# Two steps of a hand-written order moved: the loads of a later pair of images, and the mean of a group norm

## The chip, the cores and the metric

The kernel runs on one core of one Trainium2 chip. The metric is device time in microseconds of one execution; before the change it is 2930.93 us, the median of 3 runs (2928.26 to 2932.24). The core's engines have their own instruction queues and run side by side: TensorE (PE; its weight loads, PEld, are listed apart), VectorE (DVE), ScalarE (ACT) and GpSimd (POOL). SyncE (SP) issues every data transfer (DMA) of this kernel.

## The reference, cut to what matters

The input is 64 images of 1024 channels, 14 x 14 pixels, in float32. Two bottleneck blocks follow each other. The first is three convolutions with batch norms. The second, with which the change is concerned, is for each image:

```
out = relu(group_norm(conv1x1(x, w1)))                 # 1024 -> 256 channels, "first norm"
om = conv3x3(out, w_off) + b_off                       # 27 channels: 18 offsets, 9 masks
sampled = bilinear_sample(out, grid + offsets) * sigmoid(om[:, 18:])
out = einsum('bckhw,ock->bohw', sampled, w2)           # 9 taps, 256 -> 256, "second conv"
out = relu(group_norm(out))                            # "second norm"
out = group_norm(conv1x1(out, w3))                     # 256 -> 1024, "third conv", "third norm"
return relu(out + x)
```

A group norm's mean and variance go over all pixels of an image and a group of channels (32 channels in the third norm). All 1024 channels are held as 8 blocks of 128 partitions.

## The kernel before, in words

The 64 images are worked on in 32 pairs (`NP`). The first bottleneck has three stages, one convolution each, for all pairs; its results go to DRAM (`h3`), one tensor for each pair. In the second bottleneck the pairs go through a pipeline written out by hand: `slot(t)` (L1783) lists the work of one turn as small steps in the list `todo`, and runs them at its end. Slot t holds work of several pairs at once:

- of pair t+1: `first_conv`, `first_norm`, `offset_conv` (L1162), `selection` (L1211), the transposes and `factors` (L1238);
- of pair t: `sampling`, on PE with copies on ACT, in two parts `sp[0]` and `sp[1]` (taps 0 to 4 and 5 to 8), and the second conv in two parts `pd[0]` (35 products) and `pd[1]` (28);
- of pair t-1: the second norm, the third conv `d3` (28 products) and the third norm, in three steps `mean`, `root`, `end`;
- of pair t-2 and t-1: the output, in halves, with `store` (L1746);
- of pair t+2: its loads, `load` (L1069), and `residual` (L1075), the end of the first bottleneck for that pair.

`put(steps, extra, at)` (L1765) places each step of `extra` ahead of the step of `steps` with the number in `at`; `weave` (L1760) mixes two lists evenly. In a full slot (t from 2 to 30) the order is: the first conv of t+1 with `extra` (among it, at place 6, the list `late`); then `sp[0]` woven with half of `d3`; then two products of `d3`, the six steps of the offset conv and the one of `selection` (`om`); then `sp[1]` woven with the rest of `d3`; then `pd[0]` with a second list `extra`, and `pd[1]` with a third.

What sets the order of instructions: the second bottleneck fixes by hand only PE's order, which is the order of the steps. For DVE, ACT, POOL and SP the program's scheduler lays out each queue ahead of time: of the instructions that it takes as ready it places the one that was traced first. An instruction in `tc.keep_in_program_order(...)` is pinned: it can't be placed ahead of the instruction that was traced last before it on its engine. It says nothing about what is traced after it. On the chip each queue then runs in its order.

The pieces that the prediction's steps touch:

- The third norm's statistics are bn_stats on DVE (L987). `stats(3)` at the end of `d3` issues the last four, and the very last is pinned. `Norm.mean` (L1005) sums them on DVE (`total`, L1003, tile `gn_0m`), multiplies the sum by a constant matrix on PE (L1012), copies the result (L1014, `gn_0gm`) and forms the variance's terms on DVE (L1019 to L1026, `gn_0v`). `Norm.root` (L1028) multiplies those on PE (L1031), adds epsilon on DVE (L1036) and takes the power on POOL (L1037).
- The second conv multiplies seven sums of inputs instead of eight. Products (5, k) read b22, (0, k) b11, (4, k) b21, then (1, k) b12, (2, k) b22, (3, k) b11, (6, k) b21, in that order; k goes over the taps. The sums are formed in place on DVE by `subtract` (L1466, profiled as L1467): `first_sum` (L1472) makes b12 - b11, pinned; behind product (5, 4), the fifth of `pd[0]`, comes b22 - b12; behind (4, 1) b22 - b11, behind (1, 1) b21 - b22.
- `load(p)` makes four DMAs on SP, each pinned: two of x (L196) into the buffer `Y[p % 4]`, two of `h3` (L204) into `Z0`. `residual(p)` reads both: eight DVE instructions (L216), pinned, and eight relus on ACT (L228).
- `selection` issues on SP: the offsets and the mask to DRAM (L1221, L1222, tile `dm`), then three transfers that read them back, spread over partitions (L1234, tiles `wt` and `mk`). `factors` reads these on DVE (L1246), and later sends `wd` (L1266).
- `output` adds x on DVE (L1724), takes the relu on ACT (L1726) and stores (L1752). The third conv of the next pair writes the same two z buffers: on POOL (L1652) and on DVE (L1656, L1660).

Of the kernel before, what the change touches and what calls it, by code (L numbers as in the profile page):

```python
# [44 lines left out]
def kernel(  # L45
# [20 lines left out]
    NP = B // 2  # L66
# [126 lines left out]
    def load_x(p, order=lambda ins: ins):  # L193
        for i in range(2):
            order(
                nc.sync.dma_start(  # L196
                    Y[p % 4][:, :, ts(i, HW)], x[2 * p + i].rearrange("(b p) q -> p b q", p=P)
                )
            )

    def load_h3(p, r, order=lambda ins: ins):
        for half in range(2):
            order(
                nc.sync.dma_start(  # L204
                    r[:, ts(half, HB)].rearrange("p b q -> p (b q)"), h3[p][:, ts(half, HB * N2)]
                )
            )
# [447 lines left out]
    with l0, tc.manual_schedule(  # L655
# [107 lines left out]
        for p in range(2, NP - 2, 2):  # L763
            tt = Ts
            for j in range(HB):
                acc = [ps.tile([P, N2], FP, tag=f"ps{m}", name=f"c3_{p}_{j}_{m}") for m in range(4)]
                part = ts(j, P)
# [156 lines left out]
    def build_second_bottleneck(l1, path, run, early):  # L924
# [141 lines left out]
        def start(p):  # L1066
            pairs[p] = {"y": Y[p % 4]}

        def load(p):  # L1069
            start(p)  # L1070

            load_x(p, tc.keep_in_program_order)
            load_h3(p, Z0, tc.keep_in_program_order)

        def residual(p):  # L1075

            for b in range(CB):

                tc.keep_in_program_order(end_of_first(p, Z0, b))
                relu_of_first(p, b)  # L1080
# [236 lines left out]
        def spread_rows(p, e):  # L1317

            q = pairs[p]
            k0, k1 = tapsets[e]  # L1320
            S = one.tile([QR, wide * KT[e % 2]], FP, tag=f"S{e % 2}", name=f"S_{p}_{e}")
            q["S"][e] = S
            for g, r0, piece in pieces(e):
                yield nc.sync.dma_start(
                    S[:, piece],
                    q["wd"][g][0, r0 : r0 + R, k0:k1, :]
                    .rearrange("r k n -> r (k n)")
                    .unsqueeze(1)
                    .to_broadcast([R, W, piece.stop - piece.start]),
                )  # L1330
# [36 lines left out]
        def corners(p, e):  # L1367

            q = pairs[p]
            S, X = q["S"][e], q["X"][e]  # L1370
            k0, k1 = tapsets[e]
            q["S"][e] = {}
            for g, r0, piece in pieces(e):

                tc.keep_in_program_order(
                    nc.vector.tensor_tensor(S[:, piece], S[:, piece], X(piece), ALU.mult)  # L1376
                )
                q["S"][e][g, r0] = S[:, piece].rearrange("q (k i n) -> q k i n", k=k1 - k0, i=2)
# [87 lines left out]
        def subtract(dst, a, b):  # L1466
            return nc.vector.tensor_tensor(dst, a, b, ALU.subtract)  # L1467

        def sevenfold(p):
            return shared and p < NP - 1  # L1470

        def first_sum(p, e):  # L1472

            if sevenfold(p):
                kt = tapsets[e][1] - tapsets[e][0]
                b11, b12 = (pairs[p]["sm"][e][:, 0, :kt, i] for i in range(2))

                tc.keep_in_program_order(subtract(b12, b12, b11))
# [238 lines left out]
        def output(p, half):  # L1717

            q = pairs[p]
            for b in range(half * HB, half * HB + HB, 2):  # L1720
                z = q["z"][half][:, ds(b % HB, 2)]

                tc.keep_in_program_order(
                    nc.vector.tensor_tensor(z, z, q["y"][:, ds(b, 2)], ALU.add)  # L1724
                )
                nc.scalar.activation(z, z, AF.Relu)  # L1726
            store(p, half * HB, half * HB + HB)
# [55 lines left out]
        def slot(t):  # L1783


            this, ahead, back = (0 <= n < NP for n in (t, t + 1, t - 1))
            E = len(tapsets)

            def part(yes, stage, *args):
                return stage(*args) if yes else []  # L1790


            front = ahead and not (early and t < 1)
            sp = [part(this, sampling, t, e) for e in range(E)]
            pd = [part(this, second_conv, t, e) for e in range(E)]
            d3 = part(back, third_conv, t - 1)

            for e in range(2, E):
                sp[e - 2].append(lambda e=e: this and (list(spread_rows(t, e)), list(spread_columns(t, e)), corners(t, e)))
            d1 = part(front and not (early and t < 2), first_conv, t + 1)  # L1800
            norm1, norm2, norm3 = (
                part(front, first_norm, t + 1)[2 if early and t == 1 else 0 :],
                part(back, second_norm, t - 1),
                part(back, third_norm, t - 1),
            )
            weights = [lambda e=e: corners(t, e) for e in range(2)] if this else []

            late = [lambda: output(t - 2, 1)] if t >= 2 else []
            if t + 2 < NP and not (early and t < 1):
                late.append(lambda: load(t + 2))  # L1810
            if this and not d1 and not early:
                weights[0]()
            if t == NP - 1:
                ends2 = second_norm(t)
            om = part(front, offset_conv, t + 1) + part(front, selection, t + 1)
            half = len(d3) // 2
            if d1:
                extra = list(zip((5, 8, 12, 12, 13, 13, 14), norm2)) + [(10, w) for w in weights[:1]]
                extra = sorted(extra + [(6, s) for s in late], key=lambda v: v[0])
                todo = put(d1, [s for _, s in extra], [k for k, _ in extra])  # L1820
                todo += put(weave(sp[0], d3[:half]), norm1, (4, 7, 14, 16, 18, 21))
                todo += weights[1:] + d3[half : half + 2] + om
                todo += weave(sp[1], d3[half + 2 :])
            else:
                extra = list(zip((3, 6, 8, 9, 10, 10, 10), norm2)) + list(zip((0, 0, 1, 1), norm1))
                extra = sorted(
                    extra + [(9, w) for w in weights[1:]] + [(4, s) for s in late], key=lambda v: v[0]
                )
                todo = put(sp[0], [s for _, s in extra], [k for k, _ in extra])
                todo += om + weave(sp[1], d3[:half]) + d3[half:]  # L1830
            more = t + 2 < NP and not (early and t < 1)

            scale = lambda k: k * len(pd[0]) // 35
            extra = [(4, s) for s in norm3[:1]] + ([(4, lambda: first_sum(t, 0))] if this else [])
            extra += list(zip((6, 11, 16, 21), part(ahead, transposes, t + 1)))
            extra += list(zip((12, 19), part(ahead, factors, t + 1)))
            extra += list(zip((10, 20), norm3[1:]))
            extra += [(20, lambda: first_sum(t, 1))] if this and E == 2 else []
            extra += [(21, lambda: residual(t + 2))] if more else []
            extra = [(scale(k), s) for k, s in extra]  # L1840
            extra.sort(key=lambda v: v[0])
            todo += put(pd[0], [s for _, s in extra], [k for k, _ in extra])
            for e in range(1, E - 1):
                todo += sp[e + 1] + pd[e]
            if ahead:
                todo += [lambda: list(spread_rows(t + 1, 0)), lambda: list(spread_columns(t + 1, 0))]
                todo += [lambda: list(spread_rows(t + 1, 1)), lambda: lend(t + 1)]
            if early and t == 0:
                todo.append(weight_sums)

            n = len(pd[E - 1])
            extra = []
            if early and t == 0:

                extra += list(zip((5, 8), first_norm(2)))
            if early and t + 1 in (1, NP - 1):
                extra.append((12, lambda: corners(t + 1, 0)))
            if back:
                extra.append((n * 18 // 28, lambda: output(t - 1, 0)))
            if t == NP - 1:  # L1860

                extra += list(zip([n // 2 + k for k in (3, 5, 6, 6)], ends2))
            extra.sort(key=lambda v: v[0])
            todo += put(pd[E - 1], [s for _, s in extra], [k for k, _ in extra])
            if ahead:
                todo.append(lambda: list(spread_columns(t + 1, 1)))
            if back and t == NP - 1:
                todo.append(lambda: output(t - 1, 1))
            for step in todo:
                step()  # L1870
# [176 lines left out]
```

## Time and profile before

| What | Value |
|---|---|
| time, median of 3 runs | 2930.93 us |
| profiled execution, its own time | 2930.46 us |
| span of that execution in the trace | 2928.7 us |
| busy: PE, weight loads, DVE, ACT, POOL | 96%, 70%, 80%, 46%, 34% |
| one slot, from mean to mean of the third norm (1922.38, 1981.69, 2040.45) | 59.3 and 58.8 us |
| queue of SP's transfers | 421.71 MB, 44.7% of 16 DMA engines' span |

All rows but the first come from one profiled execution. The span is the time between the first and the last event that the trace shows; the execution's own time is 1.8 us longer. In a row of the trace's timeline stand: start in us from the span's start, length in us, engine, line of the kernel, operation, output <- inputs, shape, number of instructions that are merged into the row, and in brackets idle time of the engine before it and what ended it. A product of the second conv is two records of PE. Tile names lose their buffer number. A waits row reads: engine, tile and line that waited <- what it waited for: microseconds in total, times, the longest. The records on PEld are the loads of the stationary operand, which can run while PE multiplies.

### The profile page before, as it was taken

What the parts mean: (1) busy time and instruction counts of PE and PEld (TensorE: products, weight loads), DVE (VectorE), ACT (ScalarE), POOL (GpSimd) and SP (SyncE); (2) the same over time, 40 slices, a digit from 0 to 9 for tenths busy, and PEclk for the clock granted to TensorE, in tenths of its full rate; (3) what the DMA queues carried; (4) which work ended last, traced back from release to release, by engine and by line L of the source; (5) the groups of instructions that cost most, each with busy time, mean ns of one, the idle gap of its engine ahead of it and who ended that gap; (6) DMA issues with size and microseconds to landing.
All of it is one profiled execution on the core that took longest, in us unless ns stands there. A gap on an engine that the chain in (4) does not pass through costs nothing.

```text
span 2928.7 us, 40983 instructions
## 1 busy us (share of the span) xinstructions
PE 2824.3 (96%) x13327; PEld 2053.4 (70%) x13327; DVE 2330.2 (80%) x5573; ACT 1336.8 (46%) x2723; POOL 988.9 (34%) x1065
## 2 busy tenths in 40 slices
PE   9999899999999889999999999999999999999986
PEld 5555555555555468878887888778877887788773
DVE  7877899997888758778877887787878787877764
ACT  0000222114555435555555556555655565556553
POOL 4621466654666112222222222222222222222221
PEclk9999999999999999999999999999999999999998
DMA  7665000005555444564456545554555455544521
GB/s 229 192 176 154 15 1 1 1 2 213 218 195 203 133 130 138 176 187 160 141 173 184 162 143 168 188 164 144 164 187 169 142 164 185 172 142 159 183 93 46
DMA packets 350436, 424.42 MB, mean 145 GB/s; under 512 B 27876, under 2 KB 292612, under 8 KB 349956
## 3 DMA queue, kind: packets, MB, share of 16 engines
q1 hardware_dynamic: 350212, 421.71, 44.7%
q8 instruction: 107, 1.75, 0.3%
q14 instruction: 117, 0.96, 0.1%
HBM read 296.63 MB, written 116.76 MB: 141 GB/s over the span
## 4 chain that ended last, share of the span: by engine, by line
PE 63%; DVE 19%; DMA 8%; ACT 3%; POOL 3%; issue 2%; SPq 1%; DVEq 0%; ACTq 0%; POOLq 0%
PE pd L1511 18%; PE c L389 10%; PE c L770 9%; PE sp L1396 6%; PE d L1092 6%; PE c L534 5%; DMA out_dram<-z 5%; PE d L1640 4%; DVE v L520 3%; DVE gn_0st L987 2%; DVE S L1376 2%; DMA X<-wd 1%; DVE V L1647 1%; DVE off L1207 1%; DVE X L1156 1%
## 5 line engine op out<-in xcount | busy, mean ns | idle before, releaser
L1396 PE MATMUL sp<-S,aT 126*128 126x420 f32 (+3 forms) x1536 | 494.7, 419 | 22.6 <-ACT sm L1404 13.0
L1511 PE MATMUL pd<-sm,w2b_sb 128*128 128x196 f32 x2232 | 408.6, 331 | 3.8 <-DVE sm L1467 3.8
L1404 ACT COPY sm<-sp 128x336 f32<-128x336 f32 (+3 forms) x640 | 285.6, 451 | 254.5 <-PE sp L1396 239.9
L1511 PEld LDWEIGHTS pd<-sm,w2b_sb 128*128 128x128 f32 x2232 | 370.6, 190 | 4.1 <-DVE sm L1467 4.1
L1092 PE MATMUL d<-h,w1b_sb 128*128 128x392 f32 x1024 | 358.0, 498 | 2.8 <-ACT h L228 2.8
L534 PE MATMUL c<-v,u_sb 128*128 128x392 f32 x1024 | 342.9, 497 | 10.4 <-DVE bn1sh L167 8.2
L1511 PE MATMUL pd<-sm,Sc 128*128 128x196 f32 x1674 | 315.5, 331 | 0.0
L534 PEld LDWEIGHTS c<-v,u_sb 128*128 128x128 f32 x1024 | 194.4, 191 | 158.9 <-DVE v L520 11.7
L1396 PEld LDWEIGHTS sp<-S,aT 126*128 126x128 f32 x1536 | 256.7, 191 | 47.0 <-ACT sm L1404 32.4
L1467 DVE TENSOR_TENSOR sm<-sm 128x980 f32<-128x980 f32 (+1 forms) x248 | 263.4, 1072 | 20.7 <-PE pd L1511 14.6
L1511 PEld LDWEIGHTS pd<-sm,Sc 128*128 128x128 f32 x1674 | 277.9, 190 | 0.2
L1092 PEld LDWEIGHTS d<-h,w1b_sb 128*128 128x128 f32 x1024 | 188.6, 190 | 121.0 <-ACT h L228 5.2
L1707 ACT ACTIVATE z<-z,gn_0sh,gn_0sc 128x196 f32<-128x196 f32 x496 | 222.5, 537 | 36.6 <-DVE gn_0sh L1053 36.6
L1037 POOL TENSOR_TENSOR gn_0sc<-gn_0sc,mhalf 128x16 f32<-128x16 f32 (+3 forms) x35 | 122.1, 3488 | 251.6 <-DVE gn_0sc L1036 242.3
L520 DVE TENSOR_TENSOR v<-t 128x392 f32<-128x392 f32 x256 | 193.1, 812 | 0.0
L1640 PE MATMUL d<-h,w3b_sb 128*128 128x196 f32 x744 | 180.4, 333 | 0.0
L1726 ACT ACTIVATE z<-z 128x784 f32<-128x784 f32 x124 | 103.1, 855 | 145.4 <-DVE z L1724 145.2
L1652 POOL TENSOR_TENSOR E<-V,E 128x196 f32<-128x196 f32 x124 | 74.4, 600 | 281.3 <-DVE V L1647 281.3
L1640 PEld LDWEIGHTS d<-h,w3b_sb 128*128 128x128 f32 x744 | 132.9, 189 | 50.4 <-issue 19.7
L1376 DVE TENSOR_TENSOR S<-S,X 126x840 f32<-126x840 f32 (+1 forms) x192 | 148.3, 822 | 24.1 <-DMA X<-wd 18.7
L1540 POOL TENSOR_TENSOR E<-V,E 128x196 f32<-128x196 f32 x31 | 18.8, 605 | 412.7 <-DVE V L1539 392.7
L987 DVE BATCH_NORM_STATS2 gn_0st<-z 128x6 f32<-128x196 f32 x504 | 153.2, 348 | 4.2 <-ACT z L1691 0.9
(842 smaller groups left out, 5147.3 us busy)
## 6 DMA issues: line engine op xcount, KB each, us to landing
xc<-in_x_dram SPq DMA_DIRECT2D x128, 392.0 KB
h<-o SPq DMA_DIRECT2D x64, 784.0 KB
h<-in_x_dram SPq DMA_DIRECT2D x64, 784.0 KB
h<-h SPq DMA_DIRECT2D x64, 784.0 KB
out_dram<-z SPq DMA_DIRECT2D x126, 392.0 KB
S<-wd SPq DMA_DIRECT2D x64, 413.4 KB
X<-wd SPq DMA_DIRECT2D x64, 413.4 KB
S<-wd SPq DMA_DIRECT2D x64, 330.8 KB
```

The source lines that it names most:

```text
L389: nc.tensor.matmul(acc[m], a, b, start=(j == 0), stop=(j == HB - 1))
L520: nc.vector.tensor_tensor(v[:, u].rearrange("p (i y x) -> p i y x", y=7, x=7), cols[c][:, :, i : i + 13 : 2, :], cols[c][:, :, j : j + 13 ...
L534: nc.tensor.matmul(m[u], u_sb[:, c, u, k % 4, ts(o, P)], vts[k][c][:, u], start=(c == 0), stop=(c == MB - 1),)
L770: nc.tensor.matmul(planes(acc[m]), a, b, start=start, stop=True, skip_group_check=True)
L987: last = nc.vector.bn_stats(self.st[:, b, i, :], src[:, ts(i, HW)])
L1092: nc.tensor.matmul(q["pt"][o], w1b_sb[:, c, ts(o, P)], q["y"][:, c, :], start=(c == 0), stop=(c == CB - 1),)
L1396: nc.tensor.matmul(pt[:, i], q["aT"][:, i0 + i, c, starts.index(r0), :], q["S"][e][g, r0][:, :, i0 + i, :], start=(j == 0), stop=(j == len ...
L1404: nc.scalar.copy(dst, pt.rearrange("p i k n -> p k i n"))
L1467: return nc.vector.tensor_tensor(dst, a, b, ALU.subtract)
L1511: nc.tensor.matmul(bank[:, m % 2], a[:, k], b[:, k - k0],  start=(k == 0 and m in (5, 0, 2, 6)), stop=(k == T - 1), skip_group_check=True,)
L1640: nc.tensor.matmul(bank[:, m % 2 if m < 6 else 1], a, b, start=(m < 6), stop=True, skip_group_check=True)
L1707: nc.scalar.activation(z[:, ts(i, HW)], z[:, ts(i, HW)], AF.Identity, bias=n.sh[:, b, i : i + 1], scale=n.sc[:, b, i : i + 1],)
```

## The change

Two things are moved. The loads of pair t+2 leave the list `late`, which a full slot places in the first conv of pair t+1, and go to the end of `om`, so that they are traced behind the transfers of `selection`. In the list `extra` of `pd[0]`, the first step of the third norm, its mean, goes from place 4 to place 5. In the line of this second edit `first_sum(t, 0)` keeps place 4; the list is sorted by place afterwards, and the sort keeps the order of equals.

```diff
             late = [lambda: output(t - 2, 1)] if t >= 2 else []
-            if t + 2 < NP and not (early and t < 1):
-                late.append(lambda: load(t + 2))
+
+            loads = [lambda: load(t + 2)] if t + 2 < NP and not (early and t < 1) else []
...
-            om = part(front, offset_conv, t + 1) + part(front, selection, t + 1)
+            om = part(front, offset_conv, t + 1) + part(front, selection, t + 1) + loads
...
-            extra = [(4, s) for s in norm3[:1]] + ([(4, lambda: first_sum(t, 0))] if this else [])
+            extra = [(5, s) for s in norm3[:1]] + ([(4, lambda: first_sum(t, 0))] if this else [])
```

## The prediction

> **What bounds the kernel now.** I began with the page: TensorE (PE) is busy for 96% of the span, at full granted clock almost throughout. So a microsecond counts only where PE stands still. The table of stages then gives, for 1104 to 2862 us (the second bottleneck's steady slots, columns: stretch, sum, then busy PE, weight loads, VectorE, ScalarE, GpSimd):
>
> ```profile
> 1104.00:2862.00 1758.00, 1725.57 (x9777) 1411.96 (x9776) 1385.88 (x3759) 1004.29 (x2111) 460.11 (x567) 1.00 0.51 162
> ```
>
> Of 1758 us PE stands 32. The waits of PE over 1100 to 2870, and those of its weight loads, say for whom:
>
> ```profile
> PE gn_0p L1012 <- DVE gn_0m L1003: 9.9, 30, 0.9
> PE sp L1396 <- ACT sm L1404: 8.0, 31, 0.3
> PE sp L1396 <- DVE h L1542: 7.2, 1, 7.2
> PE d L1640 <- DVE z L1656: 6.5, 10, 1.2
> ```
>
> The first is the mean of the third norm, once in each of 30 slots: the change's second edit. The last is the third conv, and in 19 slots VectorE (DVE) itself waited there for a store: "DVE z L1656 <- DMA out_dram<-z" is 12.3 us in all. That is what the first edit can reach. The other two it can't. So I read one slot closely. PE's order in time around the mean:
>
> ```profile
> 1979.90 1.49 PE L1511 MATMUL pd<-sm,Sc 128*128 128x196 f32 x8
> 1981.69 0.39 PE L1012 MATMUL gn_0p<-gn_0m,grp_sb 128*128 128x16 f32 x2 [0.30 <-DVE gn_0m L1003]
> 1981.94 0.58 PE L1511 MATMUL pd<-sm,Sc 128*128 128x196 f32 x2
> 1982.35 0.49 PE L1511 MATMUL pd<-sm,w2b_sb 128*128 128x196 f32 x2
> ```
>
> Four products (two records each, 0.332 us a product) precede the mean. Without a wait it would start at 1979.90 + 4 x 0.332 = 1981.23 and hold PE 0.14 (as the root's matmul, L1031, does further down: it starts at 1984.23, the product behind it at 1984.37); really the next product starts at 1981.94, so the stall costs 0.57 us a slot. DVE in the same place:
>
> ```profile
> 1980.79 0.63 DVE L987 BATCH_NORM_STATS2 gn_0st<-z 128x6 f32<-128x196 f32 x2
> 1981.45 0.18 DVE L1003 TENSOR_TENSOR gn_0m<-gn_0st 128x16 f32<-128x16 f32 x1
> 1982.13 0.17 DVE L1014 COPY gn_0gm<-gn_0p 128x16 f32<-128x16 f32 x1 [0.49 <-PE gn_0p L1012]
> ...
> 1983.17 0.17 DVE L1026 TENSOR_TENSOR gn_0v<-gn_0q 128x16 f32<-128x16 f32 x1
> 1983.26 2.46 DVE L1467 TENSOR_TENSOR sm<-sm 128x980 f32<-128x980 f32 x2
> ```
>
> The two L1467 are `first_sum` (b12 - b11) and the difference b22 - b12 that the second conv's fifth product releases. They stand behind the whole mean because `first_sum` is pinned behind the instruction traced before it, and that is now the mean's last one, L1026.
>
> **Part one: the mean one product later.** The list `extra` is sorted by place and keeps order among equals. Now both entries have place 4 and the mean comes first. After the change it is `first_sum` at 4, mean at 5. So `first_sum` is pinned only behind the last bn_stats (L987), and is traced ahead of L1003. Only PE's order is written by hand here; on DVE the program's scheduler puts whatever is ready, earliest traced first. A row shows how it treats a ready rival:
>
> ```profile
> 1971.57 0.35 DVE L1196 TENSOR_TENSOR om<-om,om 32x196 f32<-32x196 f32 x1
> 1971.86 0.35 DVE L987 BATCH_NORM_STATS2 gn_0st<-z 128x6 f32<-128x196 f32 x1
> 1972.13 0.34 DVE L1197 TENSOR_TENSOR om<-om,om 32x196 f32<-32x196 f32 x1
> ```
>
> L1196 is traced earlier than the statistics beside it and cuts in before the last of them. And L1197, which overwrites what L1196 reads, lets one statistic pass: a dependent instruction is not ready at the moment its forerunner leaves the engine. Both points speak for the order: statistics, `first_sum` (its data are long there, L1003 still depends on the statistics), then L1003 (b22 - b12 depends on `first_sum`), then b22 - b12 in the gap in which L1014 waits for PE.
>
> Working, in the times of this slot. L1003 ends at 1981.45 + 1.17 (one L1467, mean 1174 ns) + 0.03 + 0.18 = 1982.83; the mean's matmul starts 0.06 later (as now) at 1982.90, the next product 0.25 later at 1983.15. That next product is the sixth, which now starts at 1982.35 and is followed at once, without the 0.08 that the product after a mean takes longer: PE is 0.87 behind. Second, the root (L1031) comes five products later instead of six: 1983.15 + (1984.23 - 1981.94) - 0.33 = 1985.11. Its operand: b22 - b12 runs 1982.87 to 1984.05, then L1014 to L1026 take 1.21 (1982.13 to 1983.34), ending 1985.29. A new wait of 0.24, plus 0.11 because the weights behind a stalled small matmul come late (0.25 against 0.14): 0.35. Sum 1.2 us a slot, 36 us in 30 slots. Queued behind `first_sum` on DVE are L1003 and its chain, and for that PE waits; later work has slack, as DVE is 79% busy. Bounds: the edit as intended, with L1003 still first, gains one product, 0.33 x 30 = 10 us (not the whole 17 of the stall); with both subtractions first it costs 1.17 more at the mean, nothing at the root, 2.06 x 30 = 62.
>
> The Trainium skill, TensorE: Matmul & The Clock Gate, Part 2 (step by step), says that weight loads may be pulled ahead of running matmuls while matmuls keep their order. By that the mean's weights, a constant, would be in place and a stall would end with the matmul. The trace has the load waiting too ("PEld gn_0p L1012 <- DVE gn_0m L1003", 19.2 us, 30 times: 0.64 against PE's own 0.33). By the rule each stalled matmul is 0.11 cheaper: 30 x 0.11 = 3 us off the forecast. I take the row.
>
> **Part two: the loads.** Nothing is added; four DMAs (two of x, two of h3, 784 KB each, 3.2 MB) move on SP past the three kinds of selection transfers:
>
> ```profile
> 1951.12 0.93 SPq L1752 DMA_DIRECT2D out_dram<-z  x2
> 1952.14 7.37 SPq L196 DMA_DIRECT2D h<-in_x_dram  x2
> 1959.56 2.89 SPq L204 DMA_DIRECT2D h<-h  x2
> 1974.51 0.29 SPq L1221 DMA_DIRECT2D dm<-off  x1
> ...
> 1977.82 0.79 SPq L1234 DMA_DIRECT2D mk<-dm  x1
> 1989.65 3.01 SPq L1266 DMA_DIRECT2D wd<-wt  x4
> ```
>
> What it frees: the store issued at 1951.12 shares the DMA engines with the loads, and L1656 waits for it. The weight-load waits on L1656 are 24.4 us in 30 slots. Where the wait is 0.45 (slot near 2080) PE loses nothing, where it is 1.34 (1963) PE loses 0.83; so each costs what exceeds about 0.5. Added over the 30 slots that is 11 us. It all goes: the store would have its 8.7 us (2012.2 to L1053's end at 2020.8) nearly alone. What is late next there is L1053, already counted. The selection transfers gain nothing: `wt` is there before L1246 asks.
>
> What it may cost: the loads are issued from 1978.6. Their readers are the eight L216, from 1991.75, and SP is wanted again at 1989.65. Issue takes SP 8.5 to 10.3 us now, so it just fits. The Trainium skill, DMA: Bandwidth & Descriptors, Rules for kernel authors, speaks against the edit: issue early, wait late. In the rows, traffic of the loads ends at 1968.5, 23 us before L216, so earliness is not used. By the page's HBM limit of 358 GB/s (Specifications) 3.2 MB need 9.0 us, an estimate: there at 1988. By the trace (242 to 317 GB/s while x is loaded, 349 to 389 with h3) about 11, plus one for the broadcasts ahead: 1990.6. If the whole 16.5 us from first issue to last traffic (1952.1 to 1968.5, though 1.7 MB of other traffic are in it) held again, 1995.1. Only then does L216 stall, and the L1467 behind it (1996.07) have 1.7 us before PE asks for them. I take 1990.6: no cost, and about 11 us of cover gone. If that is wrong, up to 0.4 us a slot, 12 us.
>
> **Sum.** Against the profiled execution's 2930.46 (span 2928.7 and 1.8 around it; the median 2930.93 is the same): + 36 - 11 = + 25, so 2956.
>
> **Rivals.**
> Both subtractions first (18%). If the scheduler takes b22 - b12 as ready the moment `first_sum` ends, L1003 comes last: + 62 - 11, 2981. For it: it is traced earlier. Against: the L1197 row.
> The mean stays ahead (13%), faster. If L1003 is placed before `first_sum`, both edits do what they say: - 10 - 11, 2909. For it: the stall is real and one product would cover most of it. Against: the sort and the pin. It decides on one thing, which of L1003 and L1467 comes first behind the last L987.
> The loads don't pay (12%). The store's wait stays, or L216 stalls and takes back what was won: + 36, 2967.
> The order as forecast has 51%; with the root's wait hidden it is near 2945. The last 6% are an unforeseen order of the queues that lets the edits cancel: 5 within 0.2%, 1 faster.
>
> The range takes in all but the mean that stays ahead and the tail of the dearest case: 2938 to 2984. Faster by over 0.2% 0.14, within it 0.05, slower 0.81; 0.2% (6 us) is about what a measurement of this kernel can tell from no change.
>
> **What will show it.** On DVE: L1467 directly behind the last L987, L1003 after it, the other L1467 between L1003 and L1014. On PE: the wait at L1012 up from 0.33 to about 1.1, and a new one at L1031 for L1026. On SP: L196 behind the `mk` issue at about 1978.6. No "DVE z L1656 <- DMA out_dram<-z", and no DMA wait ahead of L216. The forecast is wrong if L1003 still follows L987 directly, or if slots lengthen by a wait that isn't at L1012, L1031 or L216.

## The result, and the profile after

After the change the kernel takes 2961.32 us (median of 4 runs, 2960.36 to 2961.56), beside 2929.60 (2927.09 to 2932.24, 4 runs) for the kernel before: a ratio of 1.0109, interval 1.0093 to 1.0125. It is slower by 31.7 us, where 25 were forecast. The profiled execution's span is 2959.7 us, 31.0 more.

The stage of the second bottleneck, in the same columns as before (stretch, sum, busy PE, weight loads, VectorE, ScalarE, GpSimd, granted clock, DMA share, GB/s):

```profile
1104.00:2892.00 1788.00, 1731.03 (x9753) 1409.11 (x9752) 1375.88 (x3747) 994.59 (x2109) 450.20 (x566) 1.00 0.49 159
```

PE now stands 57 us of it instead of 32. Its waits over 1100 to 2890 say for whom; 28 rows like the last one, each with another buffer number (between gn_1 and gn_29), are 8.4 us together and had no row before:

```profile
PE gn_0p L1012 <- DVE gn_0m L1003: 27.0, 29, 0.9
PE sp L1396 <- DVE h L1542: 8.5, 1, 8.5
...
PE d L1640 <- DVE z L1656: 5.8, 6, 2.1
...
PE gn_26p L1012 <- DVE gn_26m L1003: 0.3, 1, 0.3
```

The third norm's mean waits 0.93 us in each slot instead of 0.33, as forecast in kind. The last row is the mean of the *second* norm (its tile is 4 wide, not 16), which stands at place 5 of the first conv; the prediction did not have it. PE in time, one slot; the five products (ten records) ahead of the first row start at 1991.82:

```profile
1994.58 0.40 PE L1012 MATMUL gn_0p<-gn_0m,grp_sb 128*128 128x16 f32 x2 [0.93 <-DVE gn_0m L1003]
1994.82 0.58 PE L1511 MATMUL pd<-sm,w2b_sb 128*128 128x196 f32 x2
...
1995.45 1.49 PE L1511 MATMUL pd<-sm,w2b_sb 128*128 128x196 f32 x8
1996.89 0.40 PE L1031 MATMUL gn_0p<-gn_0v,grp_sb 128*128 128x16 f32 x2
1997.13 0.58 PE L1511 MATMUL pd<-sm,w2b_sb 128*128 128x196 f32 x2
...
2019.19 0.39 PE L1012 MATMUL gn_16p<-gn_16m,grp_sb 128*128 128x4 f32 x2 [0.28 <-DVE gn_16m L1003]
2019.43 2.22 PE L1092 MATMUL d<-h,w1b_sb 128*128 128x392 f32 x6
```

The same places before, in the slot whose products start at 1979.90:

```profile
1982.90 1.49 PE L1511 MATMUL pd<-sm,w2b_sb 128*128 128x196 f32 x8
...
1984.37 0.58 PE L1511 MATMUL pd<-sm,w2b_sb 128*128 128x196 f32 x2
...
2006.18 2.22 PE L1092 MATMUL d<-h,w1b_sb 128*128 128x392 f32 x6
```

VectorE in the same slot of the kernel after, with the order of its queue:

```profile
1992.72 0.63 DVE L987 BATCH_NORM_STATS2 gn_0st<-z 128x6 f32<-128x196 f32 x2
1993.26 1.16 DVE L1467 TENSOR_TENSOR sm<-sm 128x980 f32<-128x980 f32 x1
1994.34 0.18 DVE L1003 TENSOR_TENSOR gn_0m<-gn_0st 128x16 f32<-128x16 f32 x1
1994.53 1.18 DVE L1467 TENSOR_TENSOR sm<-sm 128x980 f32<-128x980 f32 x1
1995.62 0.17 DVE L1014 COPY gn_0gm<-gn_0p 128x16 f32<-128x16 f32 x1
...
2001.93 0.17 DVE L1043 TENSOR_TENSOR gn_0sc<-gn_0sc,vec 128x8 f32<-128x8 f32 x1 [2.80 <-POOL gn_0sc L1037]
2002.02 1.17 DVE L1467 TENSOR_TENSOR sm<-sm 128x980 f32<-128x980 f32 x1
2003.10 0.16 DVE L1043 TENSOR_TENSOR gn_0sc<-gn_0sc,vec 128x8 f32<-128x8 f32 x1
...
2003.51 0.25 DVE L1053 TENSOR_TENSOR gn_0sh<-vec,gn_0sh 128x8 f32<-128x8 f32 x2
```

Before, the end of the third norm's scale was:

```profile
1987.77 1.17 DVE L1467 TENSOR_TENSOR sm<-sm 128x980 f32<-128x980 f32 x1
1989.74 0.24 DVE L1043 TENSOR_TENSOR gn_0sc<-gn_0sc,vec 128x8 f32<-128x8 f32 x2 [0.81 <-POOL gn_0sc L1037]
1990.02 0.18 DVE L1046 TENSOR_TENSOR gn_0sh<-gn_0gm,gn_0sc 128x16 f32<-128x16 f32 x1
1990.23 0.24 DVE L1053 TENSOR_TENSOR gn_0sh<-vec,gn_0sh 128x8 f32<-128x8 f32 x2
```

The first five rows of the kernel after are the order that was forecast: last statistics, `first_sum`, the mean's sum, b22 - b12, the copy. The last four were not foreseen. The subtractions all run one turn earlier now, relative to the norm's steps, so the queue holds b21 - b22 between the two instructions of the third norm's scale (L1043), where before it stood ahead of both. There it stands behind the first L1043, which waits for the power on POOL, and the second L1043 starts 1.17 us after the first, where before the two together took 0.24.

SP in the same slot: the loads follow the `mk` transfer directly.

```profile
1989.96 0.78 SPq L1234 DMA_DIRECT2D mk<-dm  x1
1990.79 1.16 SPq L196 DMA_DIRECT2D h<-in_x_dram  x2
1992.00 2.66 SPq L204 DMA_DIRECT2D h<-h  x2
```

**Where the 31 us are.** Take the start of the second conv's products as zero (1979.90 before, 1991.82 after) and follow PE. At the seventh product (1995.45; before 1982.90) it is at 3.63 instead of 3.00: 0.63 behind, the mean's part. At the product behind the root it is at 5.31 instead of 4.47 (1984.37): 0.84, so the root adds 0.21. At the product behind the second norm's mean it is at 27.61 instead of 26.28 (2006.18): 1.33, so that mean adds 0.49. Undisturbed slots are 59.70 us from mean to mean (the floor), before 58.35: + 1.35, 40.5 us in 30 slots. The slots' excess over that floor was 13.4 us in all and is 7.8 now, 5.6 less; ahead of the first of these means 3.3 are gained and behind the last 0.6. 40.5 - 5.6 - 3.3 - 0.6 = 31.0.

### The profile page after: what moved, and what is told of

Read it like the earlier page. It is cut to its first block, busy times and chain, and to the rows that moved or that the text cites. A ratio compares the mean times of both kernels' runs of the same rounds, so it can differ in the third digit from the quotient of the medians.

```text
span 2959.7 us, 40897 instructions
## 1 busy us (share of the span) xinstructions
PE 2833.3 (96%) x13327; PEld 2053.0 (69%) x13327; DVE 2323.1 (78%) x5573; ACT 1328.6 (45%) x2723; POOL 981.5 (33%) x1065
## 4 chain that ended last, share of the span: by engine, by line
PE 46%; DVE 24%; ACT 13%; POOL 6%; issue 6%; DMA 3%; SPq 1%; DVEq 0%; ACTq 0%; POOLq 0%
PE c L389 10%; PE c L770 9%; PE sp L1396 8%; ACT z L1707 7%; PE d L1640 6%; PE d L1092 6%; DVE v L520 6%; ACT h L228 4%; POOL gn_0sc L1037 4%; PE pd L1511 3%; DVE gn_0st L987 2%; DMA out_dram<-z 2%; DVE sm L1467 2%; PE om L1180 2%; DVE V L1647 1%
## 5 line engine op out<-in xcount | busy, mean ns | idle before, releaser
L1396 PE MATMUL sp<-S,aT 126*128 126x420 f32 (+3 forms) x1536 | 492.8, 418 | 21.8 <-ACT sm L1404 10.7
L1511 PE MATMUL pd<-sm,Sc 128*128 128x196 f32 x1674 | 308.1, 329 | 0.0
L534 PEld LDWEIGHTS c<-v,u_sb 128*128 128x128 f32 x1024 | 194.6, 191 | 159.0 <-DVE v L520 11.4
L1396 PEld LDWEIGHTS sp<-S,aT 126*128 126x128 f32 x1536 | 255.5, 190 | 45.0 <-ACT sm L1404 29.9
L1467 DVE TENSOR_TENSOR sm<-sm 128x980 f32<-128x980 f32 (+1 forms) x248 | 263.3, 1071 | 20.7 <-PE pd L1511 14.7
L1707 ACT ACTIVATE z<-z,gn_0sh,gn_0sc 128x196 f32<-128x196 f32 x496 | 222.5, 537 | 92.1 <-issue 78.8
L1037 POOL TENSOR_TENSOR gn_0sc<-gn_0sc,mhalf 128x16 f32<-128x16 f32 (+3 forms) x35 | 114.7, 3276 | 268.5 <-DVE gn_0sc L1036 257.5
```

The lines of the kernel that those rows point to most:

```text
L534: nc.tensor.matmul(m[u], u_sb[:, c, u, k % 4, ts(o, P)], vts[k][c][:, u], start=(c == 0), stop=(c == MB - 1),)
L1037: nc.gpsimd.tensor_tensor(scf, scf, mhalf[:, :U], ALU.pow)
L1396: nc.tensor.matmul(pt[:, i], q["aT"][:, i0 + i, c, starts.index(r0), :], q["S"][e][g, r0][:, :, i0 + i, :], start=(j == 0), stop=(j == len ...
L1511: nc.tensor.matmul(bank[:, m % 2], a[:, k], b[:, k - k0],  start=(k == 0 and m in (5, 0, 2, 6)), stop=(k == T - 1), skip_group_check=True,)
L1707: nc.scalar.activation(z[:, ts(i, HW)], z[:, ts(i, HW)], AF.Identity, bias=n.sh[:, b, i : i + 1], scale=n.sc[:, b, i : i + 1],)
```

## The experiments

The theory after the result: the loads gain about 11 us; the mean's edit costs some 41, all of it through the order on VectorE: 0.63 and 0.21 a slot because the mean's sum stands behind `first_sum`, 0.5 because b21 - b22 stands inside the scale. The rivals: the loads are what makes the second norm late (they put `residual`'s instructions later); the place of the matmul on TensorE is itself the loss, or too early still, so that more products ahead of the mean would cover it.

All ten kernels were timed beside the kernel before, in three groups; "before" is the median of the group.

| Kernel | us, median (lowest to highest) | before | ratio, interval | undisturbed slot, us |
|---|---|---|---|---|
| loads_only | 2916.67 (2914.58 to 2919.58) | 2931.58 | 0.9947 (0.9932 to 0.9961) | 58.34 |
| mean_only | 2972.75 (2966.80 to 2977.03) | 2931.58 | 1.0136 (1.0116 to 1.0155) | 59.70 |
| scale_pinned | 2933.97 (2930.28 to 2935.99) | 2931.58 | 1.0007 (0.9999 to 1.0015) | 59.13 |
| mean_six | 2970.15 (2967.04 to 2974.12) | 2931.58 | 1.0126 (1.0110 to 1.0143) | 60.16 |
| first_sum_three | 2951.09 (2948.44 to 2953.03) | 2929.69 | 1.0074 (1.0060 to 1.0088) | 59.54 |
| loads_pinned | 2914.55 (2913.00 to 2919.79) | 2929.69 | 0.9953 (0.9940 to 0.9966) | 58.46 |
| kept_pinned | 2910.71 (2908.44 to 2912.41) | 2929.69 | 0.9935 (0.9922 to 0.9949) | 58.37 |
| mean_kept_first | 2976.58 (2975.88 to 2979.41) | 2929.69 | 1.0164 (1.0150 to 1.0177) | 60.20 |
| kept_scale18 | 2902.42 (2899.98 to 2904.28) | 2930.92 | 0.9900 (0.9884 to 0.9916) | 57.97 |
| loads_scale18 | 2914.69 (2910.67 to 2915.89) | 2930.92 | 0.9939 (0.9925 to 0.9952) | 58.34 |

### One edit at a time

loads_only is the kernel after with the mean back at its old place:

```diff
-            extra = [(5, s) for s in norm3[:1]] + ([(4, lambda: first_sum(t, 0))] if this else [])
+            extra = [(4, s) for s in norm3[:1]] + ([(4, lambda: first_sum(t, 0))] if this else [])
```

> Only the loads move; the mean of the third norm keeps place 4, ahead of first_sum. Theory (order of DVE's queue makes the loss): VectorE's order is that of before, so no loss; the store's wait ahead of the third conv's first result goes, 3 to 11 us faster than before, about 2923. Rival (the loads, landing later, push the residual and with it the second norm's mean, 0.5 us a slot): 30 x 0.5 = 16 slower from that less 5 to 10 gained, 2935 to 2941, and the second norm's mean waits on PE in every slot as it does after the change.

mean_only is the kernel after with the loads back in `late`:

```diff
-            loads = [lambda: load(t + 2)] if t + 2 < NP and not (early and t < 1) else []
+            if t + 2 < NP and not (early and t < 1):
+                late.append(lambda: load(t + 2))
...
-            om = part(front, offset_conv, t + 1) + part(front, selection, t + 1) + loads
+            om = part(front, offset_conv, t + 1) + part(front, selection, t + 1)
```

> Only the mean moves to place 5; the loads stay where they were. Theory: the slot's floor rises by all three waits, 0.63 at the mean, 0.21 at the root, 0.52 at the second norm's mean, 1.36 x 30 = 41, about 2970, and the store's waits stay (nothing is gained there, though some of them may be covered by the new waits). Rival (second norm's wait comes from the loads): 0.84 x 30 = 25, about 2955, and no wait of PE at the second norm's mean.

The loads alone gain: 2916.67, 15 us by the medians, 11.0 by the spans of the profiled executions (2928.7 and 2917.7). The medians say more than the 3 to 11 expected. The floor of a slot is untouched (58.34); by the spans 7.8 us are gained within the 30 slots, the rest at the two ends. The store's wait over 1100 to 2890, before and in loads_only:

```profile
DVE z L1656 <- DMA out_dram<-z: 12.3, 19, 1.6
DVE z L1656 <- DMA out_dram<-z: 4.9, 7, 1.5
```

The mean alone costs 41 us, with a floor of 59.70 as in the kernel after, and with the second norm's waits (28 times, 8.4 us). So these waits come without moved loads, and the rival that blames `residual` falls. The difference of mean_only to the kernel after is 11.4 us by the medians and 11.2 by the spans: the loads are worth the same beside the mean's edit.

### The second norm's mean: b21 - b22 inside the scale

scale_pinned is the kernel after; only the two L1043 of the third norm are pinned, so that they stay behind b21 - b22, which is traced ahead of them.

```diff
-            def scale(self):
+            def scale(self, pin=lambda ins: ins):
...
-                    nc.vector.tensor_tensor(
+                    pin(nc.vector.tensor_tensor(
...
-                    )
+                    ))
...
-                n.scale()
+                n.scale(tc.keep_in_program_order)
```

> The changed kernel, with the first instructions of the third norm's scale pinned on VectorE, so that the difference b21 - b22 (1.17 us) stands ahead of that chain and not inside it. Nothing else differs on VectorE but the place of the mask's product. Theory: the scale, ScalarE's normalisation and the copy of E come about 0.4 to 1.2 us earlier, and the second norm's mean no longer waits: 0.52 x 30 = 16 faster than the changed kernel, about 2945. Rival (the loads delay the residual, or the second norm's wait follows from the stall of the third's): the same as the changed kernel, 2961.

All waits of the second norm's mean are gone, and the slot is 0.57 shorter: 59.13. That is the third term of the theory (0.5), shown by itself. In all it gained 27 us, 11 more than the 16 expected: the store's waits ahead of L1656 are gone too, and the last slot's wait of L1396 for L1542, 8.5 us in the kernel after, is 1.2. Why these two go with it was not taken apart.

### More products ahead of the mean

mean_six is the kernel after with the mean one more product later:

```diff
-            extra = [(5, s) for s in norm3[:1]] + ([(4, lambda: first_sum(t, 0))] if this else [])
+            extra = [(6, s) for s in norm3[:1]] + ([(4, lambda: first_sum(t, 0))] if this else [])
```

> The changed kernel with the mean at place 6 instead of 5, first_sum still at 4. Theory: the sum gn_0m is ready no sooner, so PE's mean starts at the same time with one product more done before it; but in VectorE's queue a second difference (b22 - b11, 1.17 us) now comes inside the mean's chain, so the root waits for it: about 1.2 x 30 = 35 slower than the changed kernel, less up to 16 if the second norm's mean is no longer late: 2980 to 2996. Rival (the place on PE is what counts, one product more of cover): 0.33 x 30 = 10 faster than the changed kernel, 2951.

The waits of PE over the stage:

```profile
PE gn_0p L1031 <- DVE gn_0v L1026: 41.0, 30, 1.7
PE gn_0p L1012 <- DVE gn_0m L1003: 17.4, 29, 0.6
```

One more product does shorten the mean's wait, by 0.33 a slot (27.0 / 29 to 17.4 / 29). But the root now waits 1.4 a slot (41.0 / 30). Two things make that wait: the root keeps its place and its chain starts at the mean's matmul, so the 0.33 comes back there; and a third subtraction, b22 - b11, now stands inside that chain:

```profile
2004.35 1.18 DVE L1467 TENSOR_TENSOR sm<-sm 128x980 f32<-128x980 f32 x1
2005.44 0.17 DVE L1026 TENSOR_TENSOR gn_0v<-gn_0q 128x16 f32<-128x16 f32 x1
```

L1026 starts 1.33 behind the row of L1022 (2004.11) where it started 0.30 behind it in the kernel after (1996.36 and 1996.66). That is 1.03, and with the 0.33 it is about the wait. The second norm's mean no longer waits, and the slot is 60.16, slower still. So the extra cover itself gained nothing here, and VectorE's order cost more again. The theory's size was too high (2980 to 2996).

### VectorE's order with TensorE's order unchanged

first_sum_three changes nothing on TensorE against loads_only: only `first_sum` is traced one step earlier, ahead of the mean.

```diff
-            extra = [(4, s) for s in norm3[:1]] + ([(4, lambda: first_sum(t, 0))] if this else [])
+            extra = [(4, s) for s in norm3[:1]] + ([(3, lambda: first_sum(t, 0))] if this else [])
```

> The loads stand where the change puts them, the mean's matmul stays at its old place (behind product 4), but the subtraction of the first sum is traced at place 3, so that on VectorE it stands ahead of the mean's sum: L987, L1467, L1003. Theory (it is the order on VectorE that costs, not the place on TensorE): the mean's sum comes 1.08 us later at an unchanged place of its matmul, 1.0 a slot, and the root a further 0.3 to 0.5; with 30 slots 39 to 46 us over the kernel with the loads moved alone (2916.7): 2955 to 2963. The second difference then stands ahead of the scale, so no wait of the second norm's mean. Rival (the matmul's place on TensorE costs): 2917, as with the loads moved alone.

```profile
PE gn_0p L1012 <- DVE gn_0m L1003: 37.5, 30, 1.3
```

```profile
1988.72 1.16 DVE L1467 TENSOR_TENSOR sm<-sm 128x980 f32<-128x980 f32 x1
1989.80 0.18 DVE L1003 TENSOR_TENSOR gn_0m<-gn_0st 128x16 f32<-128x16 f32 x1
...
1990.89 1.18 DVE L1467 TENSOR_TENSOR sm<-sm 128x980 f32<-128x980 f32 x1
1991.99 0.18 DVE L1020 TENSOR_TENSOR gn_0q<-gn_0q 128x32 f32<-128x32 f32 x1
```

It takes 2951.09, 34 us more than loads_only, 4 under the theory's low end and far from the rival's 2917. The mean waits 1.25 a slot instead of 0.33, and no wait of the second norm appears. So VectorE's order alone, with TensorE's unchanged, costs 1.20 us a slot (59.54 against 58.34). Of that 0.92 is the mean's wait, for one subtraction ahead of a 0.18 us sum; the rest comes at the root, where b22 - b12 now stands inside the mean's chain (the last two rows).

### The change with VectorE's old order

loads_pinned is loads_only with the scale pinned by the diff of scale_pinned.

> The loads moved, the mean at its old place, and the first two instructions of the third norm's scale kept in the order of the program on VectorE. Against the loads moved alone only the recording of a later sum (L1253) changes its place. Theory: the third norm's chain has no stall to give back here, 2908 to 2917; the lower end if the waits for the store of z (4.9 us in all) and the last slot's wait of the sp product (8.5) go as they did with the pinned scale before. Rival (pinning by itself gains 0.5 a slot, whatever stands in the chain): 2901.

kept_pinned adds to it the mean one product later, and takes the subtractions along: `first_sum` at the same place behind the mean, b22 - b12 behind the sixth product.

```diff
-                if (m, k) == (5, k1 - 1):
+                if (m, k) == ((0, k0) if e == 0 else (5, k1 - 1)):
...
-            extra = [(4, s) for s in norm3[:1]] + ([(4, lambda: first_sum(t, 0))] if this else [])
+            extra = [(5, s) for s in norm3[:1]] + ([(5, lambda: first_sum(t, 0))] if this else [])
```

> The change with VectorE's order of before: the mean's matmul behind product 5, the first sum's subtraction still behind the mean's sum (L987, L1003, L1467), the scale pinned. Theory (the matmul's place alone gives the 0.33 us of the mean's stall, some of it the root's to lose again): 10 us less than the pinned kernel with the mean at its old place, 2898 to 2910. Rival (the place on TensorE is itself the loss): 2950 to 2960.

mean_kept_first has that last diff without the pinned scale.

> As the kernel before it in this list, without the pinned scale: the subtractions stand behind the root then, and three of them with one more sum (L1246) stand inside the third norm's scale. Theory (what stands inside the scale delays the second norm's mean): the scale comes 2 to 3 us later, the second norm's mean at place 5 of the first conv waits 2 to 2.5 us a slot: 2965 to 2990. Rival (only the order around the third norm's mean counts): 2907, as with the pinned scale.

Pinning by itself gains nothing (2914.55; the slot is 0.12 longer). With VectorE's old order around the mean, the mean's later place no longer costs: kept_pinned is 2910.71, just above the expected range. Without the pin it is 2976.58, because two subtractions and L1246 enter the scale. In VectorE's rows of that kernel:

```profile
2008.61 0.24 DVE L1043 TENSOR_TENSOR gn_0sc<-gn_0sc,vec 128x8 f32<-128x8 f32 x2 [2.81 <-POOL gn_0sc L1037]
2008.77 1.17 DVE L1467 TENSOR_TENSOR sm<-sm 128x980 f32<-128x980 f32 x1
2009.86 0.97 DVE L1246 TENSOR_TENSOR wt<-wt,base_sb 126x784 f32<-126x784 f32 x1
2010.74 1.17 DVE L1467 TENSOR_TENSOR sm<-sm 128x980 f32<-128x980 f32 x1
2011.83 0.17 DVE L1046 TENSOR_TENSOR gn_0sh<-gn_0gm,gn_0sc 128x16 f32<-128x16 f32 x1
```

L1046 starts 3.2 us after the L1043 ahead of it, instead of 0.28 (1989.74 and 1990.02 before), and the second norm's mean waits 1.5 us, under the 2 to 2.5 expected. The slot is 60.20, 1.83 over that of kept_pinned; 0.5 of it is lost ahead of the first conv, among the second conv's products, whose subtractions come late too (20 of their records take 3.90 from 2009.99, in kept_pinned 3.48 from 1981.50). So a wait at the second norm grows with what stands inside the third norm's scale: no wait with nothing, 0.3 with one subtraction in it, 1.5 with two and L1246.

One thing did not come out. In kept_pinned the mean's wait is gone (1.7 us in 2 slots), yet its slot, 58.37, is no shorter than that of loads_only. Laid side by side, PE is 0.33 ahead from the mean to the first conv, and loses it at the second norm's mean. The pin holds the scale behind the weights' second sum:

```profile
1981.30 0.57 DVE L1253 TENSOR_TENSOR wt<-wt,mk 126x392 f32<-126x392 f32 x1 [0.72 <-ACT wt L1248]
1981.79 0.24 DVE L1043 TENSOR_TENSOR gn_0sc<-gn_0sc,vec 128x8 f32<-128x8 f32 x2
```

### The scale ahead of L1253

kept_scale18 is kept_pinned, and loads_scale18 is loads_pinned, with the pinned scale traced at place 18, behind b21 - b22 (17) and ahead of L1253 (19):

```diff
-            extra += list(zip((10, 20), norm3[1:]))
+            extra += list(zip((10, 18), norm3[1:]))
```

> The kernel with VectorE's old order and the mean's matmul one product later (2910.7), with the third norm's pinned scale traced at place 18 instead of 20: behind b21 - b22 (place 17), ahead of the second sum of the weights (L1253, place 19). In that kernel PE kept the 0.33 us of the mean for 22 us, up to the second norm's mean, which then came 0.37 late: L1253 held the scale back, and through it ScalarE's 16 relus, its copy of the second conv and the second norm. Theory: with L1253 behind the scale the second norm's mean comes in time, PE keeps the 0.33: a slot of 58.0 to 58.05, and 10 us less in all: 2898 to 2902. Rival (another step between the norms sets the slot): 2909 to 2912, slot 58.37.

> The control of the kernel before it in this list: the mean at its old place, the scale pinned at place 18. Theory (an earlier scale is worth something only where the mean's stall is gone): the mean's stall of 0.33 stays, slot 58.3 to 58.35, 2908 to 2916. Rival (the scale's place gains by itself): under 2905.

```profile
2031.84 0.24 DVE L1043 TENSOR_TENSOR gn_0sc<-gn_0sc,vec 128x8 f32<-128x8 f32 x2
...
2032.65 0.57 DVE L1253 TENSOR_TENSOR wt<-wt,mk 126x392 f32<-126x392 f32 x1
```

The theory held both times: 2902.42 (0.4 above its range) with a slot of 57.97, and 2914.69 with 58.34. The earlier scale is worth 0.40 a slot where PE has that much in hand (58.37 before), and 0.12 where the mean still stalls it (58.46 before), where the time is no shorter. kept_scale18 beats both kernels, by 1.0% the one before (0.9884 to 0.9916).

## Why the prediction was right, and where its sizes were off

**The order on VectorE** came out instruction by instruction as worked out from the sort, the pin and the L1196 and L1197 rows. With it both rivals of that question fell: neither did both subtractions come first, nor did the mean stay ahead. The third, that the loads don't pay, fell with loads_only. mean_only puts the edit at + 41 by itself (36 forecast). first_sum_three shows that the mechanism is the queue on VectorE: the loss comes with TensorE's order unchanged.

**The mean, 0.87 forecast, 0.63 measured.** The term that was too large is the delay of L1003. It was set at a whole subtraction and 0.03 more, 1.20. Really L1003 starts 0.97 later: 2.52 behind the products' start (1994.34) instead of 1.55 (1981.45). L1467, which doesn't depend on the statistics, follows them at 0.54 from the start of their row, where L1003, which does, followed at 0.66: 0.12 less. And L1003 starts 1.08 after L1467 does, though the record is 1.16 long: the records of neighbours in VectorE's queue overlap, as in the rows of before (1983.17 and 1983.26). The record's length was taken for its step in the queue.

**The root, 0.35 forecast, 0.21 measured.** Same term: L1014 comes 0.38 sooner than the working had it, so that only 0.11 of stall is left, and 0.10 for late weights. The waits list shows it as a wait of 0.3 in one slot only. The weight loads' own row for L1012 is 35.8 us in 29 slots, 1.23 against 0.93 on PE: the load waits with its matmul here, as the row of before had it. The Trainium skill's rule that weight loads may be pulled ahead of matmuls (TensorE: Matmul & The Clock Gate, Part 2, step by step) gave 3 us less; no run shows that saving.

**What was missed: the second norm's mean, 0.5 a slot, 15 us.** The step that failed is the sentence that for the mean's chain PE waits and "later work has slack, as DVE is 79% busy". An average share says nothing of the one chain that runs from the third norm's scale over ScalarE's 16 instructions L1707, L228, and the copy L1535 to the second norm's mean. It had no slack: L1053 ends 1.37 later in the slot (11.94 against 10.57 behind the start of the products), PE is 0.84 behind by then, and the difference, 0.53, is about the new wait's 0.49. The new order of b21 - b22 was to be had from the same rule of ready and earliest traced; it wasn't followed beyond the root. The prediction named as a sign of being wrong a wait that isn't at L1012, L1031 or L216. By its line this one is at L1012, but it is that of another norm; in what was meant, the sign came.

**The loads, 11 forecast, 11.2 measured** beside the mean's edit (spans of mean_only and after), and alone 11.0 by the spans, 15 by the medians. The forecast's 11 were to come from the slots alone; 9.9 do beside the mean's edit and 7.8 alone, the rest comes at the two ends, and why was not taken apart. What the loads might cost did not come: in the slot shown they are issued from 1990.79, in 3.9 us instead of the 8.5 to 10.3 reckoned with, and no L216 waited for a DMA in any slot. To issue early and wait late (the Trainium skill, DMA: Bandwidth & Descriptors, Rules for kernel authors) gained nothing here: the same transfers issued some 27 us later in the slot made the kernel faster, and the wait that shrank is that of a reader for the store they had stood beside. "It all goes" was too much: 8.5 us of that wait remain, in 7 slots, and 4.9 with the loads alone.

The sum: 40.5 instead of 36, with less than forecast at the third norm (0.84 for 1.2) and the missed 0.5; less 9.5 (excess and ends) instead of 11. The forecast of 2956 was 5 us low because a term too large and a term left out nearly cancelled. So the order at the third norm was foreseen, but the closeness of the sum is in part luck.

## What to carry to other kernels

Where a list is sorted by place and the queue is filled by "ready, earliest traced first", moving one step past another can swap them on every engine, as here on VectorE, not only on the one whose order was written by hand: follow each instruction whose order changes to the end of the slot, through every chain it now stands in, and ask there who waits last. A step that is moved so that work on one engine covers a wait should take along what stood behind it on the others; here the same edit is worth + 41 us or, with VectorE's order around the mean kept and the scale pinned at place 18, - 12 (2902.42 against 2914.69). For a transfer, ask what shares the DMA engines with it and has a reader waiting: here the earliest place was not the best.

## What the runs showed of the hardware

**Issue time on SP went with the traffic.** In the slot shown the four loads take SP 3.9 us to issue now (1990.79 to 1994.66), where they took 10.3 behind the store (1952.14 to 1962.45). In 2 us shortly ahead of them the DMA engines were busy 0.08 of the time now (1988 to 1990) and 0.60 before (1949 to 1951). No run varied the traffic by itself.

**The clock fell behind one stand of PE, and not behind two others.** Twice in the kernel after a store was late and PE stood for L1656 over 2 us (2.04 and 2.13). The slot with the second was 2.44 longer than the floor, that with the first 3.50. In 1 us windows behind the first (same columns; the clock is the third from the right):

```profile
1914.00:1915.00 1.00, 0.77 (x3) 0.63 (x4) 0.97 (x4) 0.74 (x2) 0.00 (x0) 1.00 0.00 0
1917.00:1918.00 1.00, 1.00 (x3) 0.58 (x2) 0.25 (x1) 0.00 (x0) 0.61 (x2) 0.50 0.00 0
```

The granted clock was 0.50 from 1916 to 1919, and PE's rows in it are longer (a pair of L1396 took 1.61 instead of 0.87). Behind the second stand, and behind one of 2.14 in kept_scale18, it stayed at 1.00; what decides is not shown.

**Why these stores are late.** In the first of these slots the `wd` transfer, on which the queue of SP waits, took longer: from the row of the last L1266 to the first L1324 4.08 us (1882.25 to 1886.33), against 2.30 in the slot ahead (1822.56 to 1824.86), and all that SP issues behind it, the stores too, moved with it. In the second it did not (2.25, from 2724.16 to 2726.41), so its store was late for another reason. Both causes stay open; no run was made on them.
